# Layer 3's attention: the softmax sums one unit later, the value bank read out first, layer 1's work between scores and values

## The chip, the cores and the metric

One core of a Trainium2 chip runs the whole program. The metric is the device time of one execution in microseconds, the median of several. Everything is float32.

## The reference, cut to what matters

The reference sends 8 images of 384 channels and 32 x 32 pixels through four residual layers: a convolutional attention (layer 0), a mixture of four experts (layer 1), a depthwise and a pointwise convolution with ternary weights (layer 2), and a deformable attention (layer 3). The change lies in the last step of layer 3, whose attention has 6 heads of 64 channels, 1024 queries and 256 sampled keys per image:

```python
q = ...                                   # 384 x 384 projection of the normalised image
off = gelu(bn(depthwise 5x5, stride 2))   # on q: gives the sampling offsets
x_s = grid_sample_bilinear(x, grid)       # 16 x 16 = 256 samples
kv = jnp.einsum('bchw,oc->bohw', x_s, kv_w)
attn = softmax(jnp.einsum('bhqd,bhkd->bhqk', qh, k) * SCALE, axis=-1)
out = jnp.einsum('bhqk,bhkd->bhqd', attn, v)
out = jnp.einsum('bchw,oc->bohw', out, proj_w) + proj_b
```

## The kernel before, in words

Layer 0 (its attention until about 1808 us of the span) and the routing of layer 1 come first, for all images. From there on, image by image, layers 2 and 3 of image b are interleaved with layer 1 of image b+1. `layers(b)` is a Python generator that runs `layer2` and then `layer3`; every `yield x` in it says "here are x microseconds of room". The loop at the end of `tile_kernel` adds these up in `due`, and whenever `due` reaches `UNIT` = 2.6 it emits one of the 48 units of `layer1(b+1)`. A unit is 3 matmuls of 128x128x512: the hidden layer (`ph`, L1260, followed by a ReLU on ScalarE and a product on VectorE) or a quarter of an output chunk (`y`, L1281; after four quarters VectorE adds it to the image, L1287). What is left of the 48 units when `layers(b)` is finished follows in one piece. For the last two images there is no layer 1 left: image 6's attention is interleaved with layers 2 and 3 of image 7, two steps of `following` for each of `this`, and the attention of image 7 stands alone.

The yields set the order in which the instructions are emitted; the Tile scheduler may still move them on their engine's queue. Each engine's queue is then fixed[...].

Layer 3's attention takes 6 units per image, one for each pair of heads `pr` and each half `h` of the queries. Of one unit:

- `scores` (L1561): four matmuls, two chunks of keys (`kc`) by two heads (`j`). A head has 64 channels, so each matmul uses 64 of the 128 rows of the array (shape 64*128), and the two heads of a chunk use different halves. ScalarE takes the exponential of each chunk (L1568), into `p`.
- the sum of the two chunks, `p01`, by GpSimd (L1592).
- `weigh` (L1577): four matmuls into `pav`; each fills 64 of the 128 columns (shape 128*64), and the two heads use different halves.
- VectorE turns `pav` into blocks of 32 x 32, `tu` (L1595).
- `pss` (L1603): two matmuls with ones, one per head, sum `p01` over the keys (shape 128*64).
- VectorE turns the sums (`ts`, L1608), takes the reciprocal (L1610), multiplies (L1611), and turns the product back into `att` (L1614).

After the 6 units come 18 matmuls of the output projection, `pf` (L1666), three output chunks, each added to the image by VectorE (L1670) and stored.

Buffers: [...]two double banks `big` (the scores, `pf`), one `vbank` (tag v), and three `fbank` (tag f: layer 1's `ph` and `y`, and the transposes). Before the change `pav` and `pss` share the one `vbank`. `pl.flat` is a set of five buffers of 128x1024 for `p`, `p01`, the sampling weights, and the chunks `o` that layer 1 of the next image loads (L1195). `om0` and `om1` hold the sampling coordinates of an image until its samples are drawn.

The emission of one unit before the change is, in short:

```python
p01 = ...; pav = weigh(pr, h, ps)
nc.vector.transpose(tu, pav)
ps = scores(*units[u + 1])        # the last unit: yield 2.0 in place of it
yield 0.5
pss = vbank(...)                  # two matmuls with ones
...                               # ts, reciprocal, product, att
yield 1.0
```

Of the kernel before, what the change touches and what calls it, by code (L numbers as in the profile page):

```python
# [9 lines left out]
ALU = mybir.AluOpType  # L10
# [3 lines left out]
N = H * W  # L14
P = 128
KC = C // P
HALF = N // 2
# [35 lines left out]
def tile_kernel(ctx: ExitStack, tc: tile.TileContext, i: dict, out: bass.AP):  # L53
    nc = tc.nc
# [895 lines left out]
    def vbank(name):  # L950
        return ps_v.tile([P, HALF], F32, tag="v", name=name)
# [422 lines left out]
    def layer3(pl, b, xt, put, general):  # L1374
# [178 lines left out]
        def scores(pr, h):  # L1553

            ps = []
            for kc in range(2):
                nm = f"3_{b}_{pr}_{h}_{kc}"
                s = big(f"s{nm}")
                for j in range(2):
                    r = slice(64 * j, 64 * j + 64)  # L1560
                    nc.tensor.matmul(  # L1561
                        s[:, j * HALF : (j + 1) * HALF],
                        lhsT=kt[r, pr, kc * P : (kc + 1) * P],
                        rhs=q[r, pr, h * HALF : (h + 1) * HALF],
                        start=True, stop=True,
                    )
                p = pl.flat([P, N], f"p{nm}")
                nc.scalar.activation(p, s, AF.Exp, scale=0.125)  # L1568
                ps.append(p)
            return ps  # L1570

        def weigh(pr, h, ps):
            pav = vbank(f"pav3_{b}_{pr}_{h}")
            for kc in range(2):
                for j in range(2):
                    hd = 2 * pr + j
                    nc.tensor.matmul(  # L1577
                        pav[64 * j : 64 * j + 64, :], lhsT=vt[:, kc, hd * 64 : (hd + 1) * 64],
                        rhs=ps[kc][:, j * HALF : (j + 1) * HALF],
                        start=(kc == 0), stop=(kc == 1),  # L1580
                    )
            return pav

        def blocks(nm):
            return pl.one([P, 16, 32], nm, f"{nm}_{b}_{pr}_{h}")

        if not general:
            ps = scores(*units[0])
            for u, (pr, h) in enumerate(units):

                p01 = pl.flat([P, N], f"p01_{b}_{u}")
                nc.gpsimd.tensor_tensor(p01, ps[0], ps[1], ALU.add)  # L1592
                pav = weigh(pr, h, ps)
                tu = blocks("tu")
                nc.vector.transpose(tu.rearrange("p a b -> p (a b)"), pav)  # L1595
                if u + 1 < NU3:
                    ps = scores(*units[u + 1])
                else:
                    yield 2.0
                yield 0.5  # L1600
                pss = vbank(f"pss3_{b}_{u}")
                for j in range(2):
                    nc.tensor.matmul(  # L1603
                        pss[64 * j : 64 * j + 64, :], lhsT=ones[:, :64],
                        rhs=p01[:, j * HALF : (j + 1) * HALF], start=True, stop=True,
                    )
                tss = blocks("ts")
                nc.vector.transpose(tss.rearrange("p a b -> p (a b)"), pss)  # L1608
                rc = rec3[:, b * NU3 + u, :]
                nc.vector.reciprocal(rc, tss[:, :, 0])  # L1610
                nc.vector.tensor_tensor(  # L1611
                    tu, tu, rc.unsqueeze(2).to_broadcast([P, 16, 32]), ALU.mult
                )
                nc.vector.transpose(  # L1614
                    att[:, pr, h * HALF : (h + 1) * HALF], tu.rearrange("p a b -> p (a b)")
                )
                yield 1.0
            yield 3.0
        else:
            for pr, h in units:  # L1620
# [273 lines left out]
```

## Time and profile before

| | |
|---|---|
| median of 3 runs | 3751.69 us (3746.74 to 3756.45) |
| the profiled execution | 3751.05 us, of which the span of the profile is 3749.3 us |
| PE busy | 3632.0 us, 97% of the span |
| VectorE busy | 1820.6 us, 49% |
| ScalarE busy | 1280.2 us, 34% |
| GpSimd busy | 199.5 us, 5% |

The attention of layer 3 starts on TensorE, in the order of the images, at 2153.3, 2380.8, 2607.9, 2835.4, 3062.5, 3290.1, 3562.2 and 3688.4 us of the span. In the first six images it takes 46.7 us until `pf` starts (15 `y` matmuls are among it), always the same within 0.02 us.

How to read it: the timeline lists instructions in order of time, merged where equal ones follow each other: start, duration, engine, line, operation, out<-in, the part of the array that is used, shape, count; in brackets idle time of the engine and what ended it. A float32 matmul is recorded as two instructions (two passes), so the four matmuls of `scores` are x8. A busy PE is not a PE at its peak: the ends of matmuls are modelled. The distance from one start to the next tells more than the duration.

### The profile page before, as it was taken

Reading aid. Unit: us, or ns where it says so; the run is one execution under the profiler, and the core shown is the slowest. Engines: PE = TensorE matmul, PEld = TensorE weight load, DVE = VectorE, ACT = ScalarE, POOL = GpSimd, SP = SyncE. Lnnn points to the kernel's source line nnn. Section 1 sums busy time; section 2 is a strip of 40 time slices with the busy share of each in tenths; the row PEclk is TensorE's granted clock in tenths of the full one; section 3 lists DMA queues with packets and bytes.
Section 4 is the critical chain, followed back from the end, with each engine's and each line's share of the span. In section 5 each row is a group of like instructions: output and inputs, shape, how many; then the busy total and the mean of one; then the engine's idle time right before and its main releaser. Section 6 shows DMA issues by size and latency. Waiting matters only on the chain.

```text
span 3749.3 us, 39325 instructions
## 1 busy us (share of the span) xinstructions
PE 3632.0 (97%) x15746; PEld 1533.0 (41%) x15746; DVE 1820.6 (49%) x2840; ACT 1280.2 (34%) x1536; POOL 199.5 (5%) x162
## 2 busy tenths in 40 slices
PE   7999999999999999999799999999999999999888
PEld 3444333333333333333244534444444444544433
DVE  6776223232323232333346557465663656547664
ACT  2222354545444454534112321323222232322222
POOL 0000100000000000000000010201001010010111
PEclk8999999999999999999899999999999999999898
DMA  6776311121212121211430000100001001010000
GB/s 198 232 251 229 131 54 36 62 63 37 63 40 75 26 72 28 71 43 55 183 140 34 17 34 17 40 28 17 34 17 51 17 17 40 19 43 17 0 34 18
DMA packets 83449, 242.49 MB, mean 65 GB/s; under 512 B 18563, under 2 KB 19091, under 8 KB 82873
## 3 DMA queue, kind: packets, MB, share of 16 engines
q1 hardware_dynamic: 70174, 200.42, 16.1%
q10 hardware_dynamic: 12504, 37.88, 3.0%
q8 instruction: 128, 2.10, 0.2%
q0 software_dynamic: 576, 1.55, 0.1%
q14 instruction: 67, 0.54, 0.0%
HBM read 122.64 MB, written 75.50 MB: 53 GB/s over the span
## 4 chain that ended last, share of the span: by engine, by line
PE 40%; DVE 9%; ACT 1%; issue 0%; DMA 0%; POOL 0%; DVEq 0%; POOLq 0%; ACTq 0%; SPq 0%
PE y L1281 11%; PE ph L1260 8%; DVE y L1355 6%; PE pq L1400 3%; PE pw L1363 3%; PE pf L1666 3%; PE s L1561 3%; PE pav L1577 2%; PE pss L1603 1%; DVE hd L1246 1%; DVE off L1470 1%; PE pk L1535 1%; PE pv L1544 1%; PE xsb L1521 1%; PE pom L1483 1%; PE plog L1023 0%
## 5 line engine op out<-in xcount | busy, mean ns | idle before, releaser
L645 ACT ACTIVATE p<-s 128x1024 f32<-128x1024 f32 x512 | 496.5, 1021 | 506.8 <-PE s L638 506.6
L1281 PE MATMUL y<-hd,w_sb 128*128 128x512 f32 x1080 | 490.2, 599 | 3.6 <-DVE hd L1246 3.6
L653 PE MATMUL pav<-p,vt 64*64 64x512 f32 x4096 | 487.0, 590 | 0.0
L1260 PE MATMUL ph<-h,w_sb 128*128 128x512 f32 x1104 | 483.3, 594 | 0.4 <-DMA w_sb<-in_w_dram 0.4
L638 PE MATMUL s<-qk,qk 48*64 48x512 f32 x3072 | 370.8, 597 | 3.3 <-ACT p L645 3.3
L391 PE MATMUL pk<-st,cw_sb 126*126 126x512 f32 x720 | 322.8, 610 | 9.5 <-DMA st<-pad 9.3
L1260 PEld LDWEIGHTS ph<-h,w_sb 128*128 128x128 f32 x1104 | 207.6, 190 | 253.5 <-issue 250.3
L1281 PEld LDWEIGHTS y<-hd,w_sb 128*128 128x128 f32 x1080 | 199.0, 191 | 249.3 <-issue 235.5
L653 PEld LDWEIGHTS pav<-p,vt 64*64 64x64 f32 x4096 | 156.6, 133 | 285.1 <-issue 285.1
L610 DVE COPY ta<-pav 128x512 f32<-128x512 f32 x64 | 44.2, 691 | 429.0 <-PE pav L653 425.9
L1355 DVE SCALAR_TENSOR_TENSOR y<-h,tap,y 128x992 f32<-128x992 f32 (+1 forms) x192 | 234.0, 1242 | 1.6
L391 PEld LDWEIGHTS pk<-st,cw_sb 126*126 126x126 f32 x720 | 140.4, 197 | 183.8 <-issue 179.1
L1470 DVE SCALAR_TENSOR_TENSOR off<-q,dw_sb,off 128x225 f32<-128x225 f32 (+3 forms) x432 | 213.1, 546 | 1.7
L1270 ACT ACTIVATE hd<-ph,b_sb 128x512 f32<-128x512 f32 x180 | 122.7, 681 | 258.6 <-PE ph L1260 258.3
L638 PEld LDWEIGHTS s<-qk,qk 48*64 48x64 f32 x3072 | 108.6, 133 | 231.1 <-issue 191.9
L78 DVE COPY qk<-pq 128x512 f32<-128x512 f32 x48 | 33.2, 691 | 292.7 <-PE pq L572 292.7
L397 ACT COPY y<-pk 126x512 f32<-126x512 f32 (+1 forms) x136 | 76.4, 583 | 255.2 <-PE pk L391 111.1
L1568 ACT ACTIVATE p<-s 128x1024 f32<-128x1024 f32 x96 | 93.1, 1021 | 173.0 <-PE s L1561 172.9
L590 PE MATMUL po<-att,wo_sb 128*128 128x512 f32 x288 | 132.8, 615 | 11.6 <-DMA att<-al 11.6
L1246 DVE TENSOR_TENSOR hd<-hd,cb 128x512 f32<-128x512 f32 x180 | 122.3, 684 | 35.5 <-ACT hd L1270 35.2
L1363 PE MATMUL pw<-y,upw 128*128 128x512 f32 x288 | 129.7, 603 | 7.6 <-DVE y L1355 7.6
L572 PE MATMUL pq<-g,wq_sb 128*128 128x512 f32 x288 | 131.2, 606 | 2.2 <-DMA wq_sb<-in_wq_dram 2.2
(280 smaller groups left out, 3961.2 us busy)
## 6 DMA issues: line engine op xcount, KB each, us to landing
g<-raw SPq DMA_DIRECT2D x72, 512.0 KB
st<-pad SPq DMA_DIRECT2D x180, 168.0 KB
raw<-y ACTq DMA_DIRECT2D x171, 168.0 KB
xa<-in_x_dram SPq DMA_DIRECT2D x24, 512.0 KB
xh<-in_x_dram SPq DMA_DIRECT2D x48, 256.0 KB
f<-in_x_dram SPq DMA_DIRECT2D x24, 512.0 KB
f<-o SPq DMA_DIRECT2D x24, 512.0 KB
o<-ot SPq DMA_DIRECT2D x42, 256.0 KB
```

What stands on the lines that cost most here:

```text
L391: nc.tensor.matmul(pk[h].rearrange("p (h w) -> p h w", w=W)[: 3 * nch, :, o0 : o0 + c1 - c0], lhsT=lhs, rhs=rhs, start=(k == 0), stop=(k = ...
L572: nc.tensor.matmul(pq, lhsT=w_in[v][:, c, pr * P : (pr + 1) * P], rhs=acts[b][v][:, c, h * HALF : (h + 1) * HALF], start=(c == 0), stop=(c ...
L590: nc.tensor.matmul(po, lhsT=wo0[:, c, m * P : (m + 1) * P], rhs=atts[b][:, c, hs], start=(c == 0), stop=(c == KC - 1),)
L638: nc.tensor.matmul(s[64 * k : 64 * k + 64, j * HALF : (j + 1) * HALF], lhsT=kt[r, k0 : k0 + 64], rhs=qt[r, h * HALF : (h + 1) * HALF], sta ...
L645: nc.scalar.activation(p, s, AF.Exp, scale=scale)
L653: nc.tensor.matmul(pav[k][64 * j : 64 * j + 64, :], lhsT=vts[b % 2][r, kc, 2 * hd : 2 * hd + 2, :].rearrange("p a b -> p (a b)"), rhs=p[r, ...
L1246: nc.vector.tensor_tensor(hd, hd, state["cb"], ALU.mult)
L1260: nc.tensor.matmul(ph, lhsT=w1[:, e, c, dc * P : (dc + 1) * P], rhs=state["h1"][c], start=(c == 0), stop=(c == KC - 1),)
L1281: nc.tensor.matmul(y, lhsT=w2[:, e, dc, m * P : (m + 1) * P], rhs=state[h, k], start=(k == 0), stop=(k == NE * KC - 1),)
L1355: nc.vector.scalar_tensor_tensor(d, f, tap2[:, c, t : t + 1], d, ALU.mult, ALU.add)
L1363: nc.tensor.matmul(pw[h], lhsT=upw2[:, c, m * P : (m + 1) * P], rhs=y[c][:, hs], start=(c == 0), stop=(c == KC - 1),)
L1470: nc.vector.scalar_tensor_tensor(d, f, dw3[:, t : t + 1], d, ALU.mult, ALU.add)
```

## The change

In units before the last, `pss` of unit u no longer follows the scores of unit u+1. It is emitted behind `weigh` of unit u+1, in `sums`, and the division behind it, in `divide`. `pss` moves from `vbank` to `fbank`, so `pav` has the single `vbank` for itself. `tu` must now live through two units: it takes `om0` and `om1` in turn. VectorE is given the transposition of the new `pav` first and the division of the unit before after it. The yields change: one `UNIT` (2.6) after the first scores and one after each unit, which lets 7 units of layer 1 into the six units of attention (and one more with the closing `yield 3.0`), where before 0.5 + 1.0 per unit and 2.0 at the last unit came to 11.0 in all, and 14.0 with the 3.0. A `yield 0.0` keeps the number of steps at 14, which counts for the interleaving of images 6 and 7.

```diff
         if not general:
-            ps = scores(*units[0])
-            for u, (pr, h) in enumerate(units):
-
-                p01 = pl.flat([P, N], f"p01_{b}_{u}")
-                nc.gpsimd.tensor_tensor(p01, ps[0], ps[1], ALU.add)
-                pav = weigh(pr, h, ps)
-                tu = blocks("tu")
-                nc.vector.transpose(tu.rearrange("p a b -> p (a b)"), pav)
-                if u + 1 < NU3:
-                    ps = scores(*units[u + 1])
-                else:
-                    yield 2.0
-                yield 0.5
-                pss = vbank(f"pss3_{b}_{u}")
+            def sums(u, p01):
+
+                pss = fbank(f"pss3_{b}_{u}")
                 for j in range(2):
                     nc.tensor.matmul(
                         pss[64 * j : 64 * j + 64, :], lhsT=ones[:, :64],
                         rhs=p01[:, j * HALF : (j + 1) * HALF], start=True, stop=True,
                     )
-                tss = blocks("ts")
+                return pss
+
+            def divide(pss, pr, h, u, tu):
+                tss = pl.one([P, 16, 32], "ts", f"ts_{b}_{u}")
                 nc.vector.transpose(tss.rearrange("p a b -> p (a b)"), pss)
                 rc = rec3[:, b * NU3 + u, :]
                 nc.vector.reciprocal(rc, tss[:, :, 0])
...
-                yield 1.0
+
+
+            ps, due3 = scores(*units[0]), None
+            yield UNIT
+            for u, (pr, h) in enumerate(units):
+                p01 = pl.flat([P, N], f"p01_{b}_{u}")
+                nc.gpsimd.tensor_tensor(p01, ps[0], ps[1], ALU.add)
+                pav = weigh(pr, h, ps)
+                if due3:
+                    pss = sums(due3[2], due3[4])
+
+                tu = pl.one([P, NG * LS], f"om{u % 2}", f"tu_{b}_{u}")[:, :HALF]
+                tu = tu.rearrange("p (a b) -> p a b", b=32)
+                nc.vector.transpose(tu.rearrange("p a b -> p (a b)"), pav)
+                if due3:
+                    divide(pss, *due3[:4])
+                due3 = pr, h, u, tu, p01
+                if u + 1 < NU3:
+                    ps = scores(*units[u + 1])
+                yield UNIT
+                yield 0.0
+            divide(sums(due3[2], due3[4]), *due3[:4])
             yield 3.0
```

More of the change, by code (lines that the diff above doesn't have):

```diff
@@ L1582, in weigh @@
             return pav
-        def blocks(nm):
-            return pl.one([P, 16, 32], nm, f"{nm}_{b}_{pr}_{h}")
         if not general:
-            ps = scores(*units[0])
-            for u, (pr, h) in enumerate(units):
-                p01 = pl.flat([P, N], f"p01_{b}_{u}")
-                nc.gpsimd.tensor_tensor(p01, ps[0], ps[1], ALU.add)
-                pav = weigh(pr, h, ps)
-                tu = blocks("tu")
-                nc.vector.transpose(tu.rearrange("p a b -> p (a b)"), pav)
-                if u + 1 < NU3:
-                    ps = scores(*units[u + 1])
-                else:
-                    yield 2.0
-                yield 0.5
-                pss = vbank(f"pss3_{b}_{u}")
+            def sums(u, p01):
+                pss = fbank(f"pss3_{b}_{u}")
                 for j in range(2):
```

## The prediction

> **What bounds the kernel now.** I read the page first (PE 97% busy, the chain that ended last mostly on PE), then the waits of PE over the six images in which layer 1 is interleaved, then PE's timeline of one attention, last the windows of the final two images.
>
> ```profile
> engine line waited for: us in total, times, longest us
> PE pw L1363 <- DVE y L1355: 4.0, 6, 0.7
> PE pav L1577 <- ACT p L1568: 2.7, 5, 0.5
> PE px L1423 <- DVE xT L78: 0.4, 2, 0.2
> ```
>
> From 2200 to 3520 us PE waits 7 us of 1320. No wait is left to remove there; only PE's own work can get shorter. That it can, PE's timeline shows (image 0, units 0 and 1):
>
> ```profile
> 2156.90 1.99 PE L1577 MATMUL pav<-p,vt 128*64 128x512 f32 x8 [0.55 <-ACT p L1568]
> 2158.82 1.99 PE L1561 MATMUL s<-q,kt 64*128 64x512 f32 x8
> 2160.74 1.08 PE L1603 MATMUL pss<-p,ones 128*64 128x512 f32 x4
> 2161.75 1.12 PE L1561 MATMUL s<-q,kt 64*128 64x512 f32 x2
> 2162.80 1.94 PE L1577 MATMUL pav<-p,vt 128*64 128x512 f32 x8
> 2164.67 1.98 PE L1561 MATMUL s<-q,kt 64*128 64x512 f32 x6
> 2166.76 1.08 PE L1603 MATMUL pss<-p,ones 128*64 128x512 f32 x4
> 2167.76 1.98 PE L1281 MATMUL y<-hd,w_sb 128*128 128x512 f32 x4
> ```
>
> Read the distances between starts. Whole scores (x8) take 2160.74 - 2158.82 = 1.92 us. The next unit's scores are torn, one matmul before `pav` and three after: (2162.80 - 2161.75) + (2166.76 - 2164.67) = 1.05 + 2.09 = 3.14 us for the same work. A lone half-array matmul has no partner beside it. Taken apart into single records, a pass of 512 columns comes 0.429 us after the one before it, whether it is one 128*128 pass or two half-array passes side by side; the first pass after a change of shape takes 0.533 us and the last one before a change 0.519 us, so a change of shape costs 0.104 + 0.090 = 0.195 us. A tear adds two passes and a change: 0.858 + 0.195 = 1.05, near the 1.22 measured, of which 0.11 is a wait for GpSimd.
>
> ```profile
> 2153.30:2200.00 46.70, 46.04 (x151) 14.40 (x151) 28.98 (x36) 15.35 (x16) 14.10 (x6) 1.00 0.11 34
> ...
> 3611.00:3657.00 46.00, 35.92 (x111) 13.03 (x109) 43.26 (x78) 8.44 (x11) 5.06 (x2) 0.94 0.09 35
> 3688.40:3742.20 53.80, 50.79 (x159) 16.52 (x158) 30.49 (x36) 13.71 (x14) 14.08 (x6) 1.00 0.05 20
> ```
>
> These windows (length, then busy PE, PEld, DVE, ACT, POOL) show image 0's attention with DVE at 29 of 46.7 us, the stretch in which image 7's 54 taps `off` (L1470) run on DVE beside image 6's attention, DVE 43.3 of 46.0, and image 7's attention alone. So PE is the bound in images 0 to 5, DVE in the second, PE and its exponentials in the third.
>
> **What the Trainium skill says.** "TensorEngine Tiling (Array Packing)", Key Properties: "Mode switching requires drain", and different tiles run in parallel. The trace agrees on both: 0.195 us per change, pairs at the price of one. "TensorE: Matmul & The Clock Gate", What overlaps and what doesn't: matmuls are strict first in, first out; so a matmul waiting for its half of the array also holds the one for the other half. The trace agrees: the lone scores matmul stays alone. "Perfetto Trace Analysis", Identifying the Most-Contended Engine: matmul busy time is no measure of nearness to the peak; here 46.0 of 46.7 us "busy" hides three tears.
>
> **The change part by part, images 0 to 5.** The built programs' instruction orders (no time is in them) give the counts. From the first scores to the end of `pf` and the y matmuls around it:
> - Before: 27 stretches of one shape, hence 26 changes; scores torn at units 2, 4 and 5. Passes: scores 24 + 3 x 2 = 30, pav 24, pss 12, y 24 matmuls x 2 = 48, pf 36: 150. 150 x 0.429 + 26 x 0.195 = 69.4; waits 0.55 + 0.11: 70.1. Measured, 2153.31 to the `w` matmul at 2223.20: 69.9. The sum closes within 0.2.
> - After: s | y | pav | s | y | pav pss | s | y | ... | y | pss | y pf: 21 stretches, no tear. pav and pss have one shape and now stand together; all 8 y units stand between scores and values, none after pf (before, 9 y matmuls stood there). 144 x 0.429 + 20 x 0.195 = 65.7, with the same 0.2 of excess 65.5.
> - The difference is 3 tears' passes (2.57), 6 changes (1.17) and the two waits (0.66): 4.4 less 0.1 for rounding, **4.3 us per image, 25.8 in six**.
>
> What hides the rest. Exponentials: pav after the first scores could start 2156.90 - 2153.31 = 3.59 us after them (a table load is in it); with y between, PE arrives after 1.92 + 2.77 = 4.69: the 0.55 goes. VectorE: a period of PE is y 2.77 + pav and pss 2.77 + s 1.92 = 7.46 us; DVE has in it two transpositions of 0.72, 0.25, the product 2.1 at worst (the product's row: 677/1969/2142 ns), 0.71, at times y's 0.75 + 0.69 and layer 1's 1.24: 7.2 at most. The product is slow only beside GpSimd's 2.35 us sum; an order in which it comes later than that sum can only shorten it. The single vbank: pav waits for `tu` of the unit before, which starts 5.5 us earlier and stands first on DVE. pss's bank: three, one held by y; freed by `ts`, a period earlier. GpSimd's sum has a whole period; the 7 waits of pss's weight loads for it (5.3 us in all, most of it covered, 0.11 us seen on PE above) fall away. The SP queue has the same order; the loads `o` sit in p buffers, whose addresses shift: `o` chunk 2 waits for pav of the last unit, lands some 3.5 us after (before: issued 2192.85, used at 2196.40), and `rec`, product and `att` of the last two units stand behind the additions of `o` on DVE. I count `att` of the last unit 8.9 us after pss of unit 4 ends; pf needs it after pss, two y units and 5 pf matmuls, 10.8 us. Covered by 2 us; uncovered, a wait of up to 3.5 us per image. pf's cover: 9 y matmuls behind it disappear, but layer 1's next `ph` hangs on `o` that came 15 us earlier. The wait `pw <- y` stays: gnb stands one matmul (0.86) earlier, but pw needs its third chunk one matmul earlier too.
> I keep 3.0 to 4.6 per image: 18 to 28.
>
> **Image 6 beside image 7.** Three terms. On PE, up to the end of image 7's pq (L1400), two passes and two changes less: -1.25. On DVE, the sums being a unit late, one more division falls behind pq, into the stretch that DVE bounds: reciprocal, product and transpositions, 2.0 as they overlap by a little (0.7 + 0.25 + 0.69 + 0.71 in single records): +2.0. DVE's new order puts xT and tu copies, which wait for px and pav on PE, before more of the taps: by passes I count 3.5 us of idle against 2 before: +1.5. **+2.3.** Bounds: -1 (no new idle) to +6 (two taps more stretched by GpSimd: one of 0.46 took 2.55).
>
> **Image 7 alone.** Before, 5.85 to 6.0 us per unit, all five scores torn. After, scores are whole except once, but the order tears pss: pav, pss, pav, pss by single heads. The trace shows no such pattern; it costs 0 to 0.86 us, and I take 0.86 since the queue is in order. s 1.92 + wait for the exponential 0.3 (0.96 + 0.1 + 1.02 + 0.1 against 1.92) + 6 passes and a change 2.77 + 0.86 = 5.85: nothing gained per unit. From the first scores: 12.5 to the scores of unit 2, 3 x 5.85 to those of unit 5, 1.92 + 0.3 + 3.63 + 0.96 to the end of pss, 18 pf matmuls 15.4: 52.3 against 53.8 (3688.4 to 3742.2). **-1.5**; bounds -5.8 and +1.
>
> **Sum.** -25.8 + 2.3 - 1.5 = -25.0. From the profiled execution's 3751.05 us (1.75 around its span): 3726.0; that run is 0.6 below the median, so 3726.5.
>
> **The rivals.**
> 1. The gain of the six images holds, the tail pays more (+6, +1): 3732 to 3735. For: DVE is full there. Inside my range. 15 in 100.
> 2. More is gained: tears and changes cost what I say, pss splits are free, tail -1: 3716. 12 in 100.
> 3. No change: the passes are saved, but PE meets new waits of about 4 us per image, at pf for `att` behind the late `o` (3.5): -25.8 + 21 + 1 = 3748. For: three DVE instructions stand behind each `o`; against: 2 us of cover. Or the tears were paid by idle time anyway; against: PE does not idle. 10 in 100.
> 4. Slower: pss now draws on the three banks that y and ph use, and its bank is freed by `ts`, behind the next `tu` on DVE. If DVE's 7.2 us grow beyond the 7.46 of a period, every sum waits. Break-even is 25/36 = 0.7 us per sum in six images; 1.0 us per sum makes it 0.3% slower; 1.5 us gives +54 - 25: 3780. For: product stretched to 2.1; against: DVE busy 29 of 46.7. 5 in 100.
>
> That the change does not do what it says is out: the built order shows whole scores in images 0 to 5.
>
> **Numbers.** My forecast has 58 in 100. About 0.3% (11 us) is what a measurement of this kernel tells from no change: faster means under 3740.4. Forecast, rivals 1 and 2 are faster: 0.85; same 0.10; slower 0.05. The range goes from the end of rival 2 (-28 - 1 - 5.8: 3716) to the bad ends together (-18 + 6 + 1: 3740).
>
> **What would show it.** Right: scores x8 in one row everywhere in images 0 to 5, 65.5 us from first scores to `w`; starts of attention 223.2 us apart instead of 227.5; the product at 0.69 us; no `pf <- att` wait before image 6. Wrong: rows `pss <- DVE ts` or `pf <- DVE att` of over 0.5 us in each image; the last tap of image 7 more than 6 us later relative to its `pw`; pss pairs in image 7 at 0.96 us though split.

## The result, and the profile after

| | before | after |
|---|---|---|
| median of 4 runs each | 3753.86 us | 3722.53 us (3718.58 to 3726.37) |
| ratio to before, 95% interval | | 0.992 (0.9906 to 0.9933) |
| profiled execution, span | 3751.05, 3749.3 us | 3726.37, 3724.5 us |
| PE, VectorE busy | 3632.0, 1820.6 us | 3605.8, 1789.3 us |

Forecast were 3726.5 us and a range of 3716 to 3740; the time is 31 us (0.8%) less than before.

Names in what follows: a pass is one of the two recorded instructions of a float32 matmul; a pair of half-array matmuls is torn when one of them stands in the queue apart from the other. `pw` (L1363) are the pointwise matmuls of layer 2, `pq` the queries, `pk` and `pv` the keys and values of layer 3. `off` are the taps, the multiply-adds of the 5x5 convolution on VectorE; `pom` (L1483) are the matmuls that turn `off` into coordinates, `xsb` and `xs` those that draw the samples, with weights `wt` from GpSimd. `w` (L1224) are the first matmuls of layer 1 behind `pf`.

The waits of PE from 2200 us to the end of the same stretch (22 us earlier than before) show that there was little to gain from waits and that little was gained; the row of `pav` for the exponential is gone:

```profile
engine line waited for: us in total, times, longest us
PE pw L1363 <- DVE y L1355: 3.7, 6, 0.6
PE px L1423 <- DVE xT L78: 0.2, 1, 0.2
```

PE's timeline of image 0, units 0 to 2, from the same 2156.90 on:

```profile
2156.90 1.99 PE L1561 MATMUL s<-q,kt 64*128 64x512 f32 x8
2158.82 2.84 PE L1281 MATMUL y<-hd,w_sb 128*128 128x512 f32 x6
2161.59 1.94 PE L1577 MATMUL pav<-p,vt 128*64 128x512 f32 x8
2163.46 1.99 PE L1561 MATMUL s<-q,kt 64*128 64x512 f32 x8
2165.37 2.84 PE L1281 MATMUL y<-hd,w_sb 128*128 128x512 f32 x6
2168.15 1.94 PE L1577 MATMUL pav<-p,vt 128*64 128x512 f32 x8
2169.91 1.03 PE L1590 MATMUL pss<-p,ones 128*64 128x512 f32 x4
2170.87 1.99 PE L1561 MATMUL s<-q,kt 64*128 64x512 f32 x8
```

No x2 and x6 are left: every unit's scores are one row of x8, and `pss` follows `pav` without a change of shape (2169.91 - 2168.15 = 1.76 us for `pav` here, 2163.46 - 2161.59 = 1.87 where scores follow). From the first scores to `w` it is 65.55 us (before 69.89).

The product of the division, before in the first fence and after in the second: count, busy us and mean ns.

```profile
L1611 DVE TENSOR_TENSOR tu<-tu,rec 128x512 f32<-128x512 f32 x48 | 74.2, 1546 | 1.5
```

```profile
L1601 DVE TENSOR_TENSOR tu<-tu,rec 128x512 f32<-128x512 f32 x48 | 33.1, 690 | 1.3
```

It comes a unit later now, and so beside no sum on GpSimd: 41 us of VectorE's time go. VectorE's busy time falls by 31 us only, since six of layer 1's additions of `o` (L1211) now do lie beside such a sum and take 2.7 to 3.0 us for 1.3. PE had waited for next to none of the 41 us (1.0 us at `pf` for `att`, beside image 7).

The windows of image 0's attention, of the stretch with image 7's `off`, and of image 7's attention (length, then busy PE, PEld, DVE, ACT, POOL, then PEclk, DMA share, GB/s):

```profile
2156.90:2207.00 50.10, 50.10 (x170) 17.32 (x170) 24.78 (x35) 14.55 (x15) 14.09 (x6) 1.00 0.10 32
3590.80:3637.30 46.50, 32.77 (x102) 12.84 (x101) 42.05 (x77) 7.98 (x9) 4.95 (x2) 0.90 0.09 35
3667.50:3717.30 49.80, 46.02 (x159) 16.78 (x158) 22.78 (x36) 13.72 (x14) 14.12 (x6) 1.00 0.05 22
```

The second still belongs to VectorE (42.05 of 46.5 us). In image 7's attention the last `pf` starts 48.66 us after the first scores (before 52.67).

### The profile page after: what moved, and what is told of

Read it like the earlier page. It is cut to its first block, busy times and chain, and to the rows that moved or that the text cites. A ratio compares the mean times of both kernels' runs of the same rounds, so it can differ in the third digit from the quotient of the medians.

```text
span 3724.5 us, 39309 instructions
## 1 busy us (share of the span) xinstructions
PE 3605.8 (97%) x15746; PEld 1530.6 (41%) x15746; DVE 1789.3 (48%) x2840; ACT 1280.7 (34%) x1536; POOL 198.9 (5%) x162
## 4 chain that ended last, share of the span: by engine, by line
PE 40%; DVE 9%; ACT 1%; issue 0%; POOL 0%; DMA 0%; DVEq 0%; POOLq 0%; ACTq 0%; SPq 0%
PE y L1281 11%; PE ph L1260 8%; DVE y L1355 6%; PE pq L1400 3%; PE pf L1677 3%; PE pw L1363 3%; PE pav L1577 2%; PE s L1561 2%; DVE hd L1246 1%; PE pss L1590 1%; PE pk L1535 1%; PE pv L1544 1%; DVE off L1470 1%; PE xsb L1521 1%; PE pom L1483 1%; PE plog L1023 0%
## 5 line engine op out<-in xcount | busy, mean ns | idle before, releaser
L1355 DVE SCALAR_TENSOR_TENSOR y<-h,tap,y 128x961 f32<-128x961 f32 (+1 forms) x192 | 234.1, 1243 | 1.6
L1363 PE MATMUL pw<-y,upw 128*128 128x512 f32 x288 | 130.2, 606 | 7.3 <-DVE y L1355 7.3
```

Source lines behind the costliest of these rows:

```text
L1355: nc.vector.scalar_tensor_tensor(d, f, tap2[:, c, t : t + 1], d, ALU.mult, ALU.add)
L1363: nc.tensor.matmul(pw[h], lhsT=upw2[:, c, m * P : (m + 1) * P], rhs=y[c][:, hs], start=(c == 0), stop=(c == KC - 1),)
```

## Where the time went, place by place

Single executions begin layer 3's attention between 2151.3 and 2157.5 us of their span, in a part that no kernel here changes. So I compare distances: from the first scores of one image to those of the next, and from image 7's first scores to the end of the span, in us.

| kernel | images 0 to 5, mean | 5 to 6 | 6 to 7 | 7 to end | median | ratio to before, 95% |
|---|---|---|---|---|---|---|
| before | 227.35 | 272.10 | 126.28 | 60.84 | | |
| after | 223.04 | 268.56 | 126.93 | 56.87 | 3722.5 | 0.992 (0.9906 to 0.9933) |
| 1 bank alone | 225.58 | 273.74 | 130.12 | 56.30 | 3743.1 | 0.9979 (0.9972 to 0.9987) |
| 2 all but the bank | 228.16 | 273.79 | 129.62 | 63.27 | 3762.2 | 1.0027 (1.0017 to 1.0037) |
| 3 scores held whole | 224.79 | 270.36 | 127.25 | 59.54 | 3737.0 | 0.9957 (0.9942 to 0.9971) |
| 4 pacing alone | 227.50 | 272.29 | 128.51 | 60.96 | 3752.2 | 1.0005 (0.9998 to 1.0012) |
| 5 all but the pacing | 226.46 | 270.89 | 125.37 | 56.83 | 3742.2 | 0.998 (0.9973 to 0.9988) |
| 6 scores by heads | 223.18 | 268.20 | 130.13 | 61.04 | 3729.8 | 0.9941 (0.9924 to 0.9958) |
| 7 sums behind scores | 223.42 | 270.29 | 133.47 | 55.84 | 3730.6 | 0.9945 (0.9927 to 0.9962) |
| 8 copies on ScalarE | 223.04 | 268.43 | 126.99 | 56.85 | 3723.0 | 0.9934 (0.9917 to 0.9951) |
| 9 as 8, pairs whole | 223.04 | 268.40 | 126.57 | 55.28 | 3720.6 | 0.9923 (0.9906 to 0.9939) |
| 10 whole pairs, adds behind taps | 223.03 | 268.59 | 126.78 | 55.28 | 3719.8 | 0.9921 (0.9908 to 0.9935) |
| 11 as 10, division late | 223.04 | 268.72 | 126.78 | 55.28 | 3720.1 | 0.9919 (0.9904 to 0.9935) |
| 12 as 10, copies on ScalarE, only image 7's scores held | 223.04 | 268.62 | 126.88 | 55.30 | 3718.1 | 0.9905 (0.9888 to 0.9921) |

The change: 5 x -4.31, then -3.54, +0.65 and -3.97: -28.4. The profiled execution after happened to start 3.6 later, hence its -24.8.

## The experiments

**1. The bank alone.** The kernel before, with `pss` in one of the three `fbank`s.

```diff
-                pss = vbank(f"pss3_{b}_{u}")
+                pss = fbank(f"pss3_{b}_{u}")
```

> The kernel before with one word changed: pss takes fbank instead of vbank; order of emission and yields stay the old ones. Theory (the shared bank makes the scheduler tear the scores; the gain is the tears and changes of shape that fall away): its order has one tear per image instead of three, 146 passes and 21 changes, and the first values wait 1.7 us for the first exponential since no y stands between: 62.6 + 4.1 + 1.7 = 68.4 us from first scores to w, against 69.9 before and 65.5 after. Starts of attention 225.8 us apart; in image 7 about 4.7 us per unit instead of 5.9. Total near 3739. Rival (the gain needs the sums to be late): no gain, 227.3 us apart, near 3754.

Measured: 3743.1 us, starts 225.58 apart, -1.77 per image of the change's -4.31. The built order, in which the scheduler is now free to put a sum ahead of the values, has one tear for three (146 passes for 150, 21 changes of shape for 26), and pays for it with waits, since nothing lies between the first scores and their values:

```profile
2152.88 1.99 PE L1561 MATMUL s<-q,kt 64*128 64x512 f32 x8
2156.47 1.08 PE L1577 MATMUL pav<-p,vt 128*64 128x512 f32 x4 [1.60 <-ACT p L1568]
2157.48 1.12 PE L1561 MATMUL s<-q,kt 64*128 64x512 f32 x2
2158.53 1.08 PE L1577 MATMUL pav<-p,vt 128*64 128x512 f32 x4
2159.54 1.98 PE L1561 MATMUL s<-q,kt 64*128 64x512 f32 x6
```

The total is 4 us above the expected 3739 because of the tail. Behind the first wait of image 5 the granted clock was 0.5 for 3.4 us, and its attention took 1.6 us longer than the others; and image 7's `pw` all stand behind image 6's first scores, as in run 7 below.

**2. All of the change but the bank.** `pss` stays in the `vbank` that it shares with `pav`.

```diff
-                pss = fbank(f"pss3_{b}_{u}")
+                pss = vbank(f"pss3_{b}_{u}")
```

> The changed kernel with one word changed back: pss in the shared vbank; late sums and new yields stay. Theory (bank): four tears per image, 152 passes, 30 changes of shape: 65.2 + 5.9 = 71.1 from first scores to w, about 1.2 more than before; starts 228.5 us apart; total 3755 to 3765, slower than before. Rival (late sums and layer 1's units between scores and values make the gain, whatever the bank): 223 to 224 us apart, total near 3725.

Measured: 3762.2 us, 0.3% slower than before. With one bank for both, `pss` cannot go right behind `pav`; the scheduler puts it into the scores that follow, and four units in six are torn:

```profile
2164.88 1.94 PE L1577 MATMUL pav<-p,vt 128*64 128x512 f32 x8
2166.74 1.12 PE L1561 MATMUL s<-q,kt 64*128 64x512 f32 x2
2167.80 1.08 PE L1590 MATMUL pss<-p,ones 128*64 128x512 f32 x4
2168.81 1.98 PE L1561 MATMUL s<-q,kt 64*128 64x512 f32 x6
```

So the rest of the change is worth +0.8 us per image without the bank and -2.5 with it (223.04 - 225.58).

**3. Only the tears removed.** The kernel before, with the scores' matmuls held in the program's order.

```diff
-                    nc.tensor.matmul(
+                    mm = nc.tensor.matmul(
...
+                    if not general:
+                        tc.keep_in_program_order(mm)
```

> The kernel before with each matmul of the scores pinned behind the one before it on TensorE, so that none is torn; pss still in vbank. Theory A (a tear is itself the loss): 144 passes, 25 changes, 0.55 of wait: 67.0 us from first scores to w, 224.5 us between starts, total near 3737. Rival B (the tear only filled the time in which TensorE waits for the shared bank): whole scores lay the wait bare, about 1 us each, 0.3 us per tear gained: 226.5 us apart, total near 3749.

Measured: 3737.0 us, starts 224.79 apart: -2.56 per image without moving a sum, a bank or a yield. In the built order no scores are torn: 144 passes, and 26 changes of shape (25 were expected), as many as before. So the 2.56 are the six passes (6 x 0.429 = 2.57). What the change has over this version, 1.75 us per image, are six changes of shape (20 for 26), 1.17 at 0.195 each and 0.95 at the prices of run 7, and the wait for the first exponential, 0.55: 1.5 to 1.7 of it.

**4. The pacing alone.** The kernel before with the change's yields only.

```diff
             ps = scores(*units[0])
+            yield UNIT
...
-                else:
-                    yield 2.0
-                yield 0.5
+                yield UNIT
...
-                yield 1.0
+                yield 0.0
```

> The kernel before with only the new pacing: the yields of layer 3's unit loop are those of the change (2.6 after the first scores, 2.6 and then nothing in each unit), sums and values stay where they were. Theory (tears and shape changes set the time): the built TensorE order of images 0 to 5 still has torn pairs and 28 shape changes for 26, so nothing is gained: starts 227 to 228 apart, 3748 to 3752 us. Rival (more of the next image's first layer between scores and values is what helps, by hiding the wait for the exponential): the 0.66 us of waits per image and part of the rest go, below 3743.

Measured: 3752.2 us, 1.0005 of before; starts 227.50 apart. The first two units are whole, the next four torn. The waits are gone, the tears are not: the passes are 150 as before (one of the four tears parts two whole pairs and costs none), the changes of shape 30 for 26 (28 were expected). Four changes more, 0.8 us, and 0.66 us of waits less are the measured +0.15.

**5. All of the change but the pacing.** The changed kernel with the yields of before.

```diff
-            yield UNIT
             for u, (pr, h) in enumerate(units):
...
-                yield UNIT
-                yield 0.0
+                if u + 1 == NU3:
+                    yield 2.0
+                yield 0.5
+                yield 1.0
```

> The changed kernel with the old pacing: sums one unit late, values turned out of their bank first, but the yields of before. Theory: the built order has 146 passes and 19 shape changes in an image's attention for 150 and 26, but the values wait for the exponential again where nothing lies between: 1.67 for the first unit and 0.27 twice by the rows of before. Per image -4 x 0.429 -7 x 0.195 +2.2 -0.66 = -1.5, so starts 225.8 apart, and images 6 and 7 as in the changed kernel: about 3738. Rival (the pacing is of no account once the sums are moved): 3723, starts 223.1 apart.

Measured: 3742.2 us, starts 226.46 apart (one of them, from image 2, 227.90; the others 225.90 and 226.30). Theory 225.8, rival 223.1. The 1.6 us of image 2 are no further wait: behind the first wait of its attention the granted clock was 0.50 (in 2610.4:2613.6; 1.00 at the same place of image 1), and its passes came 0.9 to 1.0 us apart. Without this the mean is 226.1. PE waits for exponentials again, 13.1 us in the six images and 18 times:

```profile
PE pav L1577 <- ACT p L1568: 13.1, 18, 1.6
```

So the two parts, one -0.9 (-1.2 without the slow passes of image 2) and the other +0.15 alone, give -4.31 together: the sums' place allows whole scores, and the first layer's matmuls between scores and values are what fills the wait without a tear.

One sum holds for all seven kernels: from the first scores of image 0 to `w`, passes at 0.429 us, changes of shape at 0.20 us, those into 128 rows x 64 columns at 0.15 us (run 7), and PE's waits, in us. It falls short of the measured time by 0.1 to 0.5 us everywhere:

| kernel | passes | changes (into half columns) | waits | sum | measured |
|---|---|---|---|---|---|
| before | 150 | 26 (12) | 0.66 | 69.6 | 69.9 |
| 1 bank alone | 146 | 21 (10) | 1.60 | 67.9 | 68.1 |
| 2 all but the bank | 152 | 30 (12) | 0 | 70.6 | 70.7 |
| 3 scores held whole | 144 | 26 (12) | 0.65 | 67.0 | 67.3 |
| 4 pacing alone | 150 | 30 (12) | 0.12 | 69.9 | 70.0 |
| 5 all but the pacing | 146 | 19 (8) | 2.18 | 68.2 | 68.7 |
| after | 144 | 20 (7) | 0 | 65.4 | 65.6 |

**6. Scores by heads.** The changed kernel, with the four scores' matmuls ordered head 0, head 0, head 1, head 1 and held so. Two that are next to each other in the queue now need the same half of the array.

```diff
-            for kc in range(2):
-                s = big(...)
-                for j in range(2):
+            ss = [big(...) for kc in range(2)]
+            for j in range(2):
+                for kc in range(2):
...
+                    tc.keep_in_program_order(mm)
```

> The changed kernel with the four matmuls of the scores in another order: both key chunks of head 0, then both of head 1, pinned. Theory (each half of the array takes the next matmul meant for it, even if one for the other half stands before it in the queue; the sums of image 7 looked like that): same time, 223.1 us between starts, total near 3723. Rival (strict first in, first out): 6 pass times instead of 4 for each unit's scores, +0.86 us, 5.1 per image, 228.2 us apart, total near 3757.

Measured: 3729.8 us, starts 223.18 apart, as in the changed kernel. The scores of image 0, unit 1 (first fence line) take 2161.28 - 2159.35 = 1.93 us; in strict order it would be the time of 6 passes, 2.6 us and more:

```profile
2159.35 1.99 PE L1560 MATMUL s<-q,kt 64*128 64x512 f32 x8
2161.28 2.84 PE L1281 MATMUL y<-hd,w_sb 128*128 128x512 f32 x6
```

The third matmul of the queue starts 0.013 us after the first, past the second. Strict first in, first out is out, in the form in which I used it. What this version loses against the changed kernel lies in the tail (+3.2 and +4.2). The +3.2 were not taken apart. In image 7 the scheduler put one head's sum ahead of the values and the other head's behind:

```profile
3673.48 1.99 PE L1560 MATMUL s<-q,kt 64*128 64x512 f32 x8
3675.41 1.07 PE L1591 MATMUL pss<-p,ones 128*64 128x512 f32 x2
3676.65 2.00 PE L1578 MATMUL pav<-p,vt 128*64 128x512 f32 x8 [0.17 <-ACT p L1569]
3678.48 1.02 PE L1591 MATMUL pss<-p,ones 128*64 128x512 f32 x2
3679.43 1.99 PE L1560 MATMUL s<-q,kt 64*128 64x512 f32 x8
```

A unit takes 5.95 us (3673.48 to 3679.43), 0.86 more than in the changed kernel. These 0.86 lie ahead of the values: ScalarE's first exponential starts 2.09 us after the unit's first scores here (3675.57, behind the fourth matmul) and 1.23 us after them in the changed kernel (3680.56 after 3679.33). This version in the first line, the changed kernel in the second:

```profile
3675.57 1.94 ACT L1569 ACTIVATE p<-s 128x1024 f32<-128x1024 f32 x2 [3.16 <-PE s L1560]
3680.56 1.94 ACT L1568 ACTIVATE p<-s 128x1024 f32<-128x1024 f32 x2 [3.16 <-PE s L1561]
```

The values wait for it, with the lone sum inside the wait. The other sum, for the free half, stands behind the values in the queue and did not go past them while they waited. The first scores of image 7 show the same limit. They took 2.95 us, and the other half stood empty for the first 0.96 us: the second matmul of the queue waited until then for ScalarE to empty its bank (`vt`), and the third, for the free half, did not go past it:

```profile
3667.96 0.30 PEld L1560 LDWEIGHTS s<-q,kt 64*128 64x128 f32 x4 [0.66 <-ACT vt L1548]
```

**7. Sums behind the scores.** The changed kernel, but each unit's sums come behind the next unit's scores and ahead of the first layer's matmuls.

```diff
                 pav = weigh(pr, h, ps)
-                if due3:
-                    pss = sums(due3[2], due3[4])
...
-                if due3:
-                    divide(pss, *due3[:4])
-                due3 = pr, h, u, tu, p01
                 if u + 1 < NU3:
                     ps = scores(*units[u + 1])
+                divide(sums(u, p01), pr, h, u, tu)
                 yield UNIT
```

> The changed kernel, but each unit's sums are issued behind the next unit's scores and ahead of the first layer's matmuls, not behind the next unit's values. In images 0 to 5 of the built order nothing is torn (144 passes, as in the changed kernel), but the sums no longer lie beside matmuls of their own shape: 23 shape changes in an image's attention for 20. Theory (a shape change costs 0.195 us, and nothing else differs): image starts +3 x 0.195 = +0.6, so 223.6 apart for 223.04. Rival (shape changes are not what those 0.195 are): starts within 0.2 of 223.04. In image 7 the sums now cover part of the wait for the exponential, up to 0.3 us a unit. In all about 3725.

Measured: starts 223.42 apart, +0.38 where +0.6 was expected; in images 0 to 5 nothing is torn. One unit:

```profile
2159.16 1.99 PE L1561 MATMUL s<-q,kt 64*128 64x512 f32 x8
2161.08 1.08 PE L1590 MATMUL pss<-p,ones 128*64 128x512 f32 x4
2162.09 2.84 PE L1281 MATMUL y<-hd,w_sb 128*128 128x512 f32 x6
2164.86 1.94 PE L1577 MATMUL pav<-p,vt 128*64 128x512 f32 x8
2166.73 1.99 PE L1561 MATMUL s<-q,kt 64*128 64x512 f32 x8
```

Each stretch is its passes at 0.429 and a rest: scores 1.92 - 4 x 0.429 = 0.20, y 2.77 - 6 x 0.429 = 0.20, but values 1.87 - 4 x 0.429 = 0.15 and sums 1.01 - 2 x 0.429 = 0.15. A change into the half-column shape costs 0.15, not 0.195. This kernel enters that shape four times more and y's once less than the changed one: 4 x 0.15 - 0.20 = 0.40, measured 0.38. That the price is real is shown; that it is one price was wrong. The total, 3730.6 for about 3725, has another reason: image 6 to 7 grew by 6.5 us. The scheduler put all of image 7's `pw` behind image 6's first scores, the first 9.6 us behind them (in the changed kernel the first `pw` come 14.2 us ahead of them), and the first tap of `off` on VectorE came at 55.4 for 48.2.

**8. Copies on ScalarE.** Image 7's eight copies of the transposed x (four of them on VectorE) all on ScalarE.

```diff
-                    evac(
+                    nc.scalar.copy(
                         xT[h][:, t2 + k, :]...
```

> The changed kernel with one thing more: the eight copies of image 7's transposed x out of their banks all go to ScalarE, four of them were on VectorE (4 x 0.67 us). In the built order the scores' pairs of images 6 and 7 come out whole as well (one torn pair less in each). Theory: from image 6's first scores to image 7's the taps on VectorE set the end, so 2.7 of the 126.9 us goes, and about 1 us more for the two torn pairs: 3719. Rival: the later exponentials on ScalarE take it back as waits of the values: 3722 or more.

Measured: 3723.0 us, image 6 to 7 126.99: nothing. (The torn pairs of scores are unchanged in images 6 and 7, in the records and in the built order, unlike what I had expected.) The last tap came 0.7 us earlier, at 94.05 after image 6's first scores for 94.78, of the 2.7 taken off VectorE: its last taps stand behind image 6's additions, which wait for `pf`, and `pf` waited 5.5 us for `att` where it had been 3.8. And the 0.7 us did not reach image 7: from `pom`, which follows the last tap, to image 7's first scores it is 31.83 us for 31.04, with VectorE and GpSimd as busy as before and a lower granted clock. The changed kernel first, then this version (length, then busy PE, PEld, DVE, ACT, POOL, then PEclk):

```profile
3636.55:3667.59 31.04, 26.40 (x91) 20.12 (x91) 6.08 (x11) 9.64 (x22) 4.36 (x8) 0.70 0.00 1
3630.07:3661.90 31.83, 27.18 (x91) 20.82 (x91) 6.08 (x11) 9.76 (x22) 4.36 (x8) 0.65 0.00 1
```

**9. And the pairs whole.** The same, with the scores held whole, and values and sums of image 7 held in the program's order.

```diff
+                    if last:
+                        tc.keep_in_program_order(mm)
```

(behind the matmuls of `weigh` and `sums`; for the scores as in 3)

> The same as the kernel with the eight copies on ScalarE, and in image 7 the order of values and sums is held as the program writes it, so that the two matmuls of a pair of sums lie side by side; without it four of five pairs have values between their halves. Theory (each half of the array takes the next matmul that is for it, so a matmul for the other half can go past): a split pair of sums costs nothing, so the two kernels differ by less than 1 us. Rival (strictly first in, first out): four to five splits at 0.86 us go, 3.4 to 4.3 us faster than that kernel.

Measured: 55.28 us from image 7's first scores to the end, 56.85 in version 8. Where do the 1.57 lie? The values of unit 1 start 7.83 us after the first scores, for 8.96: 1.13 from the torn scores that are whole now. From the values of unit 1 to those of unit 5, four units with four pairs of sums, split in version 8 and whole here, both need the same 20.21 us. The wait for the exponential does not hide a cost: it is 0.27 to 0.33 us in both, and from the start of the values to the next scores both take 2.78 us. The rest, 0.44, is at the end, where the order differs. The whole pairs in this version:

```profile
3675.53 1.99 PE L1579 MATMUL pav<-p,vt 128*64 128x512 f32 x8 [0.33 <-ACT p L1570]
3677.35 1.03 PE L1594 MATMUL pss<-p,ones 128*64 128x512 f32 x4
3678.31 1.99 PE L1561 MATMUL s<-q,kt 64*128 64x512 f32 x8
3680.62 1.99 PE L1579 MATMUL pav<-p,vt 128*64 128x512 f32 x8 [0.33 <-ACT p L1570]
```

A split of sums within the values costs nothing. My bound of under 1 us between the two kernels holds for the split alone.

**10 to 12. VectorE's queue at the end of image 6.** The additions of image 6's output held behind image 7's taps. The core of it (10 and 11 also hold all scores, and values and sums of image 7, as in 9; 12 has the copies on ScalarE and holds only image 7's matmuls; in 11 the list of steps is another):

```diff
-        for _ in this:
-            for _ in range(2):
+        for n, _ in enumerate(this):
+            for _ in range({26: 0, 27: 0, 28: 12, 29: 6, 30: 0}.get(n, 2)):
...
+                if last:
+                    tc.keep_in_program_order(tap)
...
+            if b == B - 2:
+                tc.keep_in_program_order(add)
```

> The changed kernel, with all pairs of scores held whole, values and sums of image 7 in the program's order, and VectorE's queue near the end of image 6 laid out by hand: image 6's last division ahead of the taps that are left, one add of image 6's output (it waits for TensorE) after 19 of the 25 taps, and the other two adds behind the last tap. In the changed kernel the last taps stand behind all three adds, and end 94.8 us after image 6's first scores though the last add waits for TensorE until then. Theory (that order, not VectorE's work, is what the stretch waits for; the copies on ScalarE gave nothing): the last tap comes at about 88, so from image 6's first scores to image 7's 120 us for 126.9, and with 1.5 us for the whole pairs about 3714. Rival (the later adds hold the third output's bank and TensorE waits for that instead, or the taps are no faster): 3721 or more.

> The same, but taps keep coming two steps at a time until the adds, so that twelve taps stand ahead of image 6's last division, and only the two later adds go behind the last tap. Theory: the last division, and with it the output projection, comes about 5 us later than in the version with the division first, and the last tap at about 89: 3715 to 3717, between that version and the changed kernel. Rival: no better than the changed kernel, 3721 or more.

> The changed kernel, with image 7's matmuls in the program's order (pairs whole), its eight copies of x on ScalarE, and VectorE's queue at image 6's end laid out by hand: the last division ahead of the last 19 taps, one add before the last 16 taps, two adds behind them. Unlike the two kernels of the batch before, TensorE's order in image 6 is left to the scheduler, so the taps need not start later (56.6 us after image 6's first scores there, 48.2 in the changed kernel). Theory: from 48 on VectorE is busy 44.2 of 47 us in the changed kernel; without the copies and the waits for TensorE the last tap comes at about 91 for 94.8, image 7's first scores at about 123 for 126.9, and 1.5 us for the whole pairs: 3717. Rival: VectorE waits elsewhere for it, 3721 or more.

Measured: 3719.8, 3720.1 and 3718.1 us, image 6 to 7 126.8 to 126.9 in all three. The theory fell three times; all that these versions have over the changed kernel is the 1.6 us of version 9 in image 7. In 12, PE's waits from 2100 us on show where the gain went:

```profile
PE pf L1685 <- DVE x L1689: 6.9, 1, 6.9
PE pf L1685 <- DVE att L1612: 4.6, 1, 4.6
```

The 7.7 us of `pom` waiting for `off` have become 6.9 of `pf` waiting for an addition to free its bank. And the last tap comes at 95.8, 95.7 and 96.0 us for 94.8, since the first comes at 56.6, 56.6 and 56.2 for 48.2. In version 12 VectorE is idle from 45.4 to 52.9 us, its first tap being queued behind `tu` of a unit of image 6 whose values PE has yet to compute; from there to the last tap it has no gap of over 0.3 us. The measured times of these versions and of the changed kernel cannot be told apart by their intervals; none is shown to be better.

## Why the prediction was right, and where not

- **What bounds the kernel; passes and tears: right.** Forecast were 4.3 us per image from three tears, six changes and two waits; measured 227.35 - 223.04 = 4.31. Runs 1 to 5 take the same sum apart: holding the scores whole gives 2.56 alone, and the pacing, which removes only the waits, gives nothing alone. Runs 2 and 3 ended within their forecasts of the time, run 4 at the edge of its own; 1 and 5 ended 4 us above theirs, 1 by its tail (5 to 6 and 6 to 7 together 5.5 us longer than before), 5 by starts 0.7 us further apart, of which the slow passes of one image make 0.3 in the mean and the lower price of changes into half columns 0.2. A tear costs its two passes; whether it also costs a change of shape depends on what stands around it (run 3 has no tear, and as many changes as before).
- **One price for a change of shape: the sum right, the price too even.** 0.195 into scores and full matmuls, 0.15 into values and sums (run 7). At these prices the six changes are 0.95 us, not 1.17.
- **The wait for `att` at `pf`, and the banks, at nothing: right.** There is no row `pf <- att` or `pss <- DVE ts` before image 6. Rival 3's 3.5 us per image did not come. Rival 4's break-even was not neared: VectorE in image 0's attention is at 24.8 us of 50.1, the product being at 0.69 us throughout.
- **Images 5 to 6: 3.54 of the 4.3.** The 4.3 us are there until image 7's first `pw` (258.66 us after image 5's first scores, now 254.38); 0.8 is given back between that and image 6's `pk`. There TensorE comes out of waits of 7.9 and 3.0 us, the same before and after, and its first passes of `pw` come at least 0.853 us apart: four before, six after the change, at a granted clock of 0.59 (3548.72:3553.25 before) and 0.50 (3526.48:3531.76 after). These two slow passes more make the 0.8. What set the moment at which the clock came back, no run tells.
- **Image 6 beside image 7: +2.3 forecast, +0.65 measured.** Term by term, from image 6's first scores: image 7's first tap comes at 48.17 us for 49.63, so PE's part was -1.46 for the forecast -1.25. From the first tap to the end of the last VectorE takes 1.57 us longer, where +3.5 was forecast, before and after:

```profile
3611.77:3656.81 45.04, 35.15 (x106) 12.56 (x102) 42.70 (x78) 7.60 (x9) 5.06 (x2) 0.94 0.09 35
3588.83:3635.44 46.61, 33.99 (x110) 13.32 (x108) 44.02 (x82) 7.57 (x9) 4.95 (x2) 0.92 0.09 34
```

Busy it is 1.3 us more (forecast 2.0 for the additional division), idle 0.25 more (forecast 1.5): the idle time is the term that was furthest off. So the last tap comes only 0.1 us later after image 6's first scores (0.85 later after its own first `pw`, of which the slow `pw` above are 0.75). The other 0.5 of the +0.65 are `pom`'s passes, of which more came at the low clock (7.7 us of waiting lie ahead of them for 6.7). PE waits new 3.8 us for `att` and 1.8 us for `tu`, none of which shows in the sum. That VectorE is the bound there, as I wrote, is half true: of 2.7 us of its work taken away 0.7 reached the last tap, and the lower clock took that back (run 8); three other orders gained nothing either. The stretch is a chain in which VectorE and PE wait for each other in turn, and a saving on one shows up as a wait of the other.
- **Image 7: -1.5 forecast, -3.97 measured; the step that failed is the 0.86 us for a split pair of sums.** It rested on the Trainium skill, "TensorE: Matmul & The Clock Gate", What overlaps and what doesn't, that matmuls are strict first in, first out. The records differ, and here the measurement decides. (That the lone scores matmul of before stayed alone, which the prediction took for agreement, says nothing on it: the next matmul in its queue has another shape.) The built queue is values of head 0 and 1 (first chunk), sum of head 0, values of head 0 and 1 (second chunk), sum of head 1; image 7, unit 1, after the change:

```profile
3676.55 1.08 PE L1577 MATMUL pav<-p,vt 128*64 128x512 f32 x4 [0.32 <-ACT p L1568]
3677.45 0.59 PE L1590 MATMUL pss<-p,ones 128*64 128x512 f32 x1
3677.47 0.64 PE L1577 MATMUL pav<-p,vt 128*64 128x512 f32 x1
3677.88 0.59 PE L1590 MATMUL pss<-p,ones 128*64 128x512 f32 x1
3677.95 0.96 PE L1577 MATMUL pav<-p,vt 128*64 128x512 f32 x2
3678.38 0.59 PE L1590 MATMUL pss<-p,ones 128*64 128x512 f32 x1
```

While the sum of head 0 holds one half (3677.45, 3677.88), a matmul of the values runs in the other (3677.47, 3677.95). It can only be head 1's, since head 0's needs the half that is taken, and head 1's stands behind head 0's in the queue. Then head 0's values run beside the sum of head 1. So it is 6 passes, not 8, and a unit takes 5.04 to 5.09 us (starts of `pav` 3676.55, 3681.64, 3686.68), not 5.85. By the prediction's own stages: 11.74 us to the scores of unit 2 for 12.5, then 3 x 5.06 for 3 x 5.85; that is 3.1 of the 3.2 us by which `pf` ends earlier than forecast (49.1 for 52.3). In the sum only 2.5 of them appear, because the 53.8 of before, from which the -1.5 was taken, reach 0.7 us past the end of `pf` (53.1 when read as the 49.1 is). Run 6 shows the same with scores, run 9 that whole pairs are no faster. This was rival 2 of the prediction for the tail, which had 3716 with an image 6 that pays nothing.

Summed: image 7 gave 2.5 more than forecast, image 6 to 7 cost 1.65 less, 5 to 6 gave 0.8 less: 3.4 us under the forecast sum. That the total came so near is the six images' doing, where the mechanism was right. The tail's two terms were both off, by 2.5 and 1.65 us the same way; they are small beside 25.8, and by luck the 0.8 of the slow passes went the other way.

## What to carry to other kernels

Where matmuls take half of the array, count passes and changes of shape from the built order, not from the source: who shares a bank with whom decides where the scheduler may put a matmul, and one that lands between the two halves of a pair costs a pass for each half. Look for whole pairs (one row of x8) in the timeline, and for work of the full shape that can fill the wait behind a pair without splitting it; here neither the place nor the filler gained much alone. On a stretch that two engines share in a chain, work taken from the busier one may reach the end of it only in part (0.7 of 2.7 us in run 8): find first the wait that ends last. And before a difference of a microsecond behind an idle stretch of TensorE is put down to the order of instructions, compare the granted clock of both traces there.

## What the runs showed of the hardware

- Two matmuls for different halves of the array need not be neighbours in the queue: one for the free half starts past one that waits for the taken half (0.013 us behind the first in run 6; 0.00 us for four split pairs in run 9). It did not go past one that waited for another engine: in run 6 the third matmul of image 7's first scores stood 0.96 us behind one that waited for ScalarE, and a sum stayed behind values that waited for their exponential.
- Changes of shape cost 0.195 us into 64 rows x 128 columns or the full array, 0.15 us into 128 rows x 64 columns, with float32 passes of 0.429 us (distances between starts in run 7).
- The 128x512 product with a broadcast factor took 0.68 to 0.70 us wherever no sum on GpSimd lay beside it: in all 48 places after the change, and in 18 of the 48 before. The 30 others of before took 1.45 to 2.14 us.
- Behind idle time of TensorE the granted clock was 0.5 in places, and passes of 512 columns came 0.853 us apart for 0.429. In runs 1 and 5 this happened behind the 1.6 us wait for the first exponential in one of six images, for 3.4 us, at a cost of 1.6 us. Ahead of image 6's attention, where TensorE waits 7.9 us for `wt`, the clock was 0.5 for 24 to 31 us in every kernel.
